# A fused macaron layer: the first unit's exponentials of its first 512 queries beside the last of its own maxima, and the opening's pieces in another order

## The chip, the cores and the metric

The kernel runs on one core of one Trainium2 chip. The metric is the device time of one execution in microseconds; before the change the median of four runs is 1354.56 us.

## The reference

Input x has 8 batches of 1024 rows of 256 values. The layer is feed-forward (a mixture of 8 experts with a capacity), attention, feed-forward, each on the normalized x and added to it:

```python
x = x + 0.5 * ffn(layernorm(x), gate_w, w1, b1, w2, b2)
x = x + attn(layernorm(x), Wq, bq, Wkv, bkv, Wo, bo)
x = x + 0.5 * ffn(layernorm(x), gate_w, w1, b1, w2, b2)

# attn: 16 heads of 16
q = x @ Wq.T + bq
k, v = split(x @ Wkv.T + bkv, 2)
dots = einsum('bhid,bhjd->bhij', q * scale, k)
dots = where(causal, MASK_VAL, dots)
out = einsum('bhij,bhjd->bhid', softmax(dots), v)
return out @ Wo.T + bo

# ffn: top 2 of 8 experts; an expert that more rows ask for than its capacity
# gives none of them anything
counts = bincount(a_e, length=E)
keep = counts <= cap
contrib = y[a_e, p] * (a_w * keep[a_e])[:, None]
```

An expert with more rows than its capacity adds nothing. The kernel counts the rows of each expert on the chip and runs a feed-forward layer only if some expert of it is kept; in the profiled execution none is, and the time is that of the attention and of the counting.

## The kernel before

**Units.** The attention works in 32 units, one for each batch `b` and group `g` of four heads: unit u = 4b + g. A unit needs the transposed queries and keys of its heads, `qT` and `kT` (128 x 1024, each head on a block of 32 partitions, 16 of them used and one more in each block holding a row of its own). There are four of each, taken in turn.

**Three kinds of work in a unit.** `m_steps(u)` gives 24 steps on the maxima: in each, for two heads (h = 0, 1), TensorE multiplies 128 queries by up to 512 keys into a score buffer `sm`, and VectorE reduces it along the row, straight with the causal mask (a custom instruction that writes `top`) or first to a partial maximum `first` where a row of blocks is wider than 512. Steps 0 to 7 are queries 0 to 511 (blocks 3, 2, 1, 0, two steps each, 512 to 128 keys wide), steps 8 to 15 the first 512 keys of queries 512 to 1023, steps 16 to 23 their remaining keys (512 to 128 wide). `settle(u, hf)` turns the maxima of one half of the queries on VectorE (`turned`), writes them to DRAM (`top_d`) and, three steps later, reads them back as one row in each block of `qT`; both are DMAs of SP, and the second waits for the first. With that row in `qT`, and -1 in the matching row of `kT` (a fill from `row16`), the products that `e_steps(u)` makes come out with the maximum taken away. `e_steps(u)` gives 24 steps also: for half 0 of the queries key blocks 0 to 3 (two steps each, 512 to 128 queries wide), for half 1 key blocks 0 to 7. In a step, for two heads, TensorE makes the products `sc`, ScalarE the exponentials into `pT`, GpSimd masks the diagonal block; two and three steps later TensorE multiplies `pT` by the values `vaug` into `pav`.

**The loop.** `for u in range(-1, NU)`: in unit u the scores of unit u lie beside the maxima of unit u + 1, a step of each at a time, so that the four row groups of TensorE hold two score and two maxima products. Stage u = -1 has only the maxima of unit 0 and takes two of their steps at a time; the last unit has only scores. All score buffers, `sm` and `sc`, come from six PSUM buffers in turn.

**Pieces.** `Beside` holds generators of further work. At every step the loop calls `beside.step(kinds)`: first whatever is due by its count of steps, then the second half of an open piece (`REST`), then the first work that asks for one of the kinds, in the order given (`QK` for projections, `PIECE` for the rest). `project(u)` makes the queries and keys of unit u: two halves of 512 rows, each two pieces of matmuls (`pq`), a copy on ScalarE (`packed`) and eight DMAs of 32 KB on SP (for unit 0 four of the eight are issued by ScalarE). `values_of(b, ...)` makes the values: two pieces of matmuls (`pv`) and two copies for each of eight blocks of 128 rows. `weights` (the generator `turning`) turns the weights: the first two parts before the loop, the gate and the value weights as first pieces, the rest in unit 0. `prepare` loads the next batch's x and takes its row statistics on VectorE.

**The opening** (lines 1142 to 1189): the loads of x in two halves of four blocks, statistics of both halves, then for each half the four normalized blocks `xn` (VectorE), two groups of four transposes (`turned`, `pta`, copied by ScalarE to `xnT`), and `project(0)` of that half. The `kT` fills of `kTs[:2]` stand before all this on ScalarE, those of `kTs[2:]` after it. Then

```python
opening = beside.add(chain(some(turning, 2), project(1), values_of(0, 0, 0, HT)))
```

and the other four blocks of values come in unit 0, ahead of all other pieces. In stage -1 there are two calls of `beside.step` after each pair of maxima steps, in unit 0 one call per step, with `(PIECE, QK)`.

**Order.** PE, VectorE, ScalarE and GpSimd compute in the order of the program (class `InOrder` ties each instruction to the one before). DMA issues are not tied: each issuing queue runs in one fixed order, which the framework chose when it built the program; in the trace the loads of the next two batches stand on SP at 9.01 us, far ahead of their place in the code. `bank` is a pair of PSUM buffers shared by `pta`, `pq`, `pv`, `pav` and the turned weights.

Of the kernel before, what the change touches and what calls it, by code (L numbers as in the profile page):

```python
# [13 lines left out]
ALU = mybir.AluOpType  # L14
# [4 lines left out]
P = 128  # L19
# [30 lines left out]
PIECE, QK, REST = "piece", "qk", "rest"  # L50


class Beside:
# [26 lines left out]
    def step(self, kinds=(), rest=True):  # L80
        self.now += 1
        self.due()
        if self.open is not None:
            if rest:
                self.advance(self.open)
            return
        for kind in kinds:
            for work in self.works:
                if work[1] == kind:
                    self.advance(work)  # L90
                    return
# [12 lines left out]
def macaron_kernel(  # L104
# [17 lines left out]
    B, S, D = x.shape  # L122
# [3 lines left out]
    TB = S // P  # L126
    DC = D // P
    NH = 16
    HD = D // NH
# [6 lines left out]
    QSCALE = HD ** -0.5  # L136
# [44 lines left out]
    row16 = const.tile([P, 1], F32, name="row16")  # L181
# [142 lines left out]
    def ln_rstd(mv, what, std=None):  # L324
        n = mv.shape[1]
        ve = norm.tile([P, TB], F32, tag="ve", name=f"ve_{what}")
        gpsimd.tensor_scalar(ve[:, :n], mv[:, :, 1], EPS, None, ALU.add)
        rstd = norm.tile([P, TB], F32, tag="rstd", name=f"rstd_{what}")
        gpsimd.tensor_tensor(rstd[:, :n], ve[:, :n], half[:, :n], ALU.pow)
        if std is not None:  # L330
            gpsimd.tensor_tensor(std, ve[:, :n], rstd[:, :n], ALU.mult)
        return rstd
# [351 lines left out]
    def attention(run_no, src, dst, gate0, logits, tally):  # L684
# [3 lines left out]
        with stack:  # L688
# [51 lines left out]
                yield 2  # L740


            def turned(b, jj, xns):
                pt = bank(f"pta{b}_{jj}")
                for i, xn in enumerate(xns):
                    for c in range(DC):
                        o = (c * 2 + i) * P
                        transpose(pt[:, o : o + P], xn[:, c * P : (c + 1) * P])
                scalar.copy(
                    xnTs[b][:, :, 2 * jj * P : (2 * jj + 2) * P], pt.rearrange("p (c w) -> p c w", c=DC)  # L750
                )

# [376 lines left out]
            def drain(steps):  # L1129
                for _ in steps:  # L1130
                    pass

            def some(steps, n):
                for _ in range(n):
                    ask = next(steps, None)
                    if ask is None:
                        return
                    yield ask
# [14 lines left out]
            qTs = [fixed.tile([P, S], F32, name=f"qT{run_no}_{k}") for k in range(4)]  # L1153
            kTs = [fixed.tile([P, S], F32, name=f"kT{run_no}_{k}") for k in range(4)]
            vaugs = [fixed.tile([P, TB, NH * VW + 32 - VW], F32, name=f"vaug{run_no}_{k}") for k in range(2)]
            gpsimd.memset(qTs[0], 0.0)
            for kT in kTs[:2]:
                scalar.copy(kT, row16.to_broadcast([P, S]))
            turning = weights(ap, bank, matmul, transpose) if gate0 is not None else iter(())
            next(turning, None)  # L1160
            next(turning, None)
# [1 line left out]
            stds[0] = norm.tile([P, TB], F32, tag="std", name="std0")  # L1163
            xnTs[0] = ap.tile([P, DC, S], F32, tag="xnT", name="xnT0", bufs=1)
            rstds = []
            for j0 in (0, HT):
                for j in range(j0, j0 + HT):
                    ln_stats(xb, j, st, mv)
                part = slice(j0, j0 + HT)
                rstds.append(ln_rstd(mv[:, part, :], f"a0_{j0}", stds[0][:, part]))  # L1170
            if gate0 is not None:
                gpsimd.tensor_scalar(bkqT[64:], bkqT[64:], QSCALE, None, ALU.mult)
            for qT in qTs[1:]:
                gpsimd.memset(qT, 0.0)
            for vaug in vaugs:
                gpsimd.memset(vaug[:, :, : NH * VW].rearrange("p t (h r) -> p t h r", r=VW)[:, :, :, HD:], 1.0)
                gpsimd.memset(vaug[:, :, NH * VW :], 1.0)
            for hf in range(2):
                xns = []
                for j in range(HT):  # L1180
                    xn = norm.tile([P, D], F32, tag="xn", name=f"xn_a0_{hf}_{j}", bufs=8)
                    ln_apply(xn, xb, hf * HT + j, mv, rstds[hf][:, j : j + 1])
                    xns.append(xn)
                for jj in range(2):
                    turned(0, 2 * hf + jj, xns[2 * jj : 2 * jj + 2])
                drain(project(0, (hf * 512,)))
            for kT in kTs[2:]:
                scalar.copy(kT, row16.to_broadcast([P, S]))
            beside = Beside()
            opening = beside.add(chain(some(turning, 2), project(1), values_of(0, 0, 0, HT)))  # L1190
            owed, adds, light, last, ons = deque(), deque(), deque(), [], {}
            STEPS = 24

# [1 line left out]
            for u in range(-1, NU):  # L1195
                b, g = divmod(u, NG)
                if u == 0:
                    beside.finish(opening)
                    preparing = beside.add(prepare(1, 2, 2))
                    opening = beside.add(values_of(0, 0, HT, TB), first=True)  # L1200
                    projecting = beside.add(project(2))
                    beside.add(chain((PIECE,), turning, residual(0)))
                if u >= 0 and g == 2 and b + 1 < B:
# [12 lines left out]
                if u > 0 and g == 0:  # L1216
                    beside.finish(valuing)
                ms = list(m_steps(u + 1)) if u + 1 < NU else [None] * STEPS
                es = list(e_steps(u)) if u >= 0 else []
                for k in range(0, STEPS, 2) if u < 0 else ():  # L1220

                    for h in range(2):
                        ms[k](h)
                        ms[k + 1](h)
                    if k == 8:
                        beside.add(settle(0, 0), first=True)
                    for _ in range(2):
                        beside.step((QK, PIECE))
                for k in range(0, STEPS, 2) if u == NU - 1 else ():

                    then = es[k + 1][1]
# [17 lines left out]
                    for kinds in ((PIECE,), ()):  # L1249
                        if light:  # L1250
                            light.popleft()()
                        beside.step(kinds)
                for k in range(STEPS) if 0 <= u < NU - 1 else ():


                    scores, then = es[k]
                    for h in range(2):
                        scores(h)
                        if ms[k] is not None:
                            ms[k](h)  # L1260
                    now = u * STEPS + k
                    if then is not None:
                        owed.append((now + 2, then, 0))
                        owed.append((now + 3, then, 1))
                    while owed and owed[0][0] <= now:
                        _, then, part = owed.popleft()
                        then(part)


                    if adds and 8 <= k <= 16:  # L1270
                        add_row()
                    if light and 8 <= k < 16 and g in (1, 2):
                        light.popleft()()
                    if u == NU - 2 and k in (0, 3):
                        beside.add(leave_first(b, k // 3))
                    if u == NU - 2 and k == 9:
                        dividing = beside.add(divided(b, 0, 8, 12, ons[0][:, 1], (2, 3, 3, 3)))
                    if g == 3 and k == 9:

                        beside.add(leave(b, 0))  # L1280
                    if g == 3 and k == 8:
                        beside.add(gate_first(b))
                    if g == 0 and b and k == 2:
                        beside.add(leave(b - 1, 1))
                    if g == 0 and b and k == 9:
                        beside.add(residual(b))
                    if g == 2 and b and k == 9:
                        beside.add(regate(b - 1, 0, TB))
                    if g == 1 and k == 7 and b + 1 < B:

                        beside.finish(preparing)
                        entering = beside.add(enter(b + 1), first=True)
                    if u == 0 and k == 15:
                        beside.finish(opening)
                    if k == 9 and ms[k] is not None:
                        beside.add(settle(u + 1, 0), first=True)
                    if k == 0:
                        settling = beside.add(settle(u, 1), first=True)
                    if k == 6:
                        beside.finish(settling)  # L1300
                    if u == 0:
                        beside.step((PIECE, QK))
                    elif g != 1 and u < NU - 2 and k not in (0, 8):

                        beside.step((PIECE,) if k in (2, 10, 13, 17) else (), k not in (14, 18))
                    elif k in (0, 8):
                        beside.step((QK, PIECE))
                    else:
                        beside.step((PIECE,) if k in long_steps or beside.pending() > 1 else ())
# [75 lines left out]
```

## Time and profile before

| | |
|---|---|
| median of 4 runs | 1354.56 us (1354.2 to 1356.48) |
| profiled execution | 1352.08 us, span 1350.20 us |
| mean granted TensorE clock | 0.989 |
| PE, matmul | 1315.1 us busy, 97% |
| DVE | 1015.4 us, 75% |
| ACT | 807.6 us, 60% |
| POOL | 440.1 us, 33% |
| first `sm` matmul (stage -1) | 24.58 us |
| first `sc` matmul (unit 0) | 52.35 us |
| first `sc` matmul of unit 0's step 8 | 68.22 us |
| first `sc` matmul of unit 1 | 99.01 us |

Times are microseconds from the start of the span. PE is TensorE's matmuls, PEld its weight loads, DVE VectorE, ACT ScalarE, POOL GpSimd, SPq the DMA issues of SyncE. Matmuls are pipelined and their ends are modelled: a matmul that waits in the queue can read as busy. A line of a timeline gives start, duration, engine, line, operation, output and inputs by name, count, and in brackets how long the engine was idle before it and what ended that. L37 is the line of the helper that records nearly every instruction, so groups are told apart by tile names.

### The profile page before, as it was taken

What the parts mean: (1) busy time and instruction counts of PE and PEld (TensorE: products, weight loads), DVE (VectorE), ACT (ScalarE), POOL (GpSimd) and SP (SyncE); (2) the same over time, 40 slices, a digit from 0 to 9 for tenths busy, and PEclk for the clock granted to TensorE, in tenths of its full rate; (3) what the DMA queues carried; (4) which work ended last, traced back from release to release, by engine and by line L of the source; (5) the groups of instructions that cost most, each with busy time, mean ns of one, the idle gap of its engine ahead of it and who ended that gap; (6) DMA issues with size and microseconds to landing.
All of it is one profiled execution on the core that took longest, in us unless ns stands there. A gap on an engine that the chain in (4) does not pass through costs nothing.

```text
span 1350.2 us, 51515 instructions
## 1 busy us (share of the span) xinstructions
PE 1315.1 (97%) x20664; PEld 437.0 (32%) x20664; DVE 1015.4 (75%) x3297; ACT 807.6 (60%) x1910; POOL 440.1 (33%) x776
## 2 busy tenths in 40 slices
PE   5999999999999999999999999999999999999994
PEld 2333333333333333333333333333333333333331
DVE  4876677778777788877778777777787777877865
ACT  3256666566666666666666666656666666666562
POOL 3034113442146221452125521354214622143321
PEclk9899999999999999999999999999999999999997
DMA  5011112212111121222122221211221111122201
GB/s 146 18 27 43 43 37 61 60 43 74 55 54 61 53 61 50 61 59 58 52 59 62 58 75 37 62 58 50 66 60 54 57 52 32 48 60 59 63 24 34
DMA packets 67024, 73.73 MB, mean 55 GB/s; under 512 B 24688, under 2 KB 42232, under 8 KB 66776
## 3 DMA queue, kind: packets, MB, share of 16 engines
q1 hardware_dynamic: 65432, 69.56, 17.8%
q8 instruction: 165, 2.70, 0.9%
q10 hardware_dynamic: 1344, 0.79, 0.2%
q14 instruction: 83, 0.68, 0.2%
HBM read 26.87 MB, written 26.20 MB: 39 GB/s over the span
## 4 chain that ended last, share of the span: by engine, by line
PE 95%; DVE 2%; issue 1%; ACT 1%; POOL 0%; DMA 0%; ACTq 0%; DVEq 0%; POOLq 0%
PE sc L37 42%; PE pav L37 24%; PE pq L37 9%; PE sm L37 8%; PE pv L37 5%; PE px L37 4%; PE pta L37 1%; DVE first L37 1%; ACT kT L37 0%; PE px_last L37 0%; DVE st_g L37 0%; ACTq L845 0%; DVE cand_g L37 0%; DVE xa L37 0%; DMA sums<-att_d 0%
## 5 line engine op out<-in xcount | busy, mean ns | idle before, releaser
L37 ACT ACTIVATE pT<-sc 128x512 f32<-128x512 f32 (+3 forms) x1536 | 669.2, 489 | 472.4 <-PE sm L37 356.2
L37 PE MATMUL sm<-kT,qT 32*64 32x512 f32 (+3 forms) x6144 | 731.4, 508 | 0.1
L37 PE MATMUL sc<-qT,kT 32*64 32x512 f32 (+3 forms) x6144 | 693.6, 507 | 0.0
L37 POOL TENSOR_SCALAR_AFFINE_SELECT pT<-pT 128x256 f32<-128x256 f32 x512 | 207.6, 407 | 786.5 <-ACT pT L37 778.9
L37 PE MATMUL pav<-pT,vaug 128*32 128x160 f32 (+4 forms) x5120 | 382.0, 370 | 2.8 <-POOL pT L37 2.0
L37 DVE TENSOR_REDUCE first<-sm 128x1 f32<-128x512 f32 x512 | 328.1, 684 | 75.1 <-PE sm L37 68.9
L37 DVE CUSTOM_DVE_ANT_0 sm<-sm,causal 128x256 f32<-128x256 f32 (+3 forms) x512 | 242.5, 516 | 131.2 <-PE sm L37 122.5
L37 DVE CUSTOM_DVE_ANT_0 sm<-sm,causal,first 128x256 f32<-128x256 f32 (+3 forms) x512 | 261.9, 557 | 84.6 <-PE sm L37 72.5
L37 PEld LDWEIGHTS sc<-qT,kT 32*64 32x64 f32 x6144 | 183.1, 130 | 368.9 <-ACT pT L37 303.7
L37 PEld LDWEIGHTS pav<-pT,vaug 128*32 128x32 f32 x5120 | 102.3, 108 | 362.2 <-issue 268.9
L37 PEld LDWEIGHTS sm<-kT,qT 32*64 32x64 f32 x6144 | 205.6, 130 | 17.7 <-DVE first L37 6.2
L37 DVE DVE_READ_ACCUMULATOR2_ANT top<- 128x1 f32 x1024 | 145.7, 142 | 0.0
L37 PE MATMUL pq<-xnT,wkqT 128*32 128x512 f32 x1024 | 137.2, 612 | 4.7 <-ACT xnT L37 3.2
L37 PE MATMUL pv<-wvT,xnT 128*32 128x264 f32 x1024 | 81.1, 392 | 0.0
L37 PE MATMUL px<-woT,on 128*32 128x264 f32 x960 | 76.2, 389 | 0.2 <-DVE xa L37 0.2
L37 POOL TENSOR_SCALAR xn_a<-xa,mv_a,rstd_a 128x256 f32<-128x256 f32 x56 | 67.8, 1221 | 0.0
L37 POOL TENSOR_TENSOR xa<-row,xa 128x264 f32<-128x264 f32 x56 | 41.8, 746 | 50.1 <-ACT row L37 50.1
L37 ACT ACTIVATE packed<-pq,bkqT 128x512 f32<-128x512 f32 x64 | 45.4, 709 | 11.1 <-PE pq L37 11.1
L37 POOL TENSOR_TENSOR xa<-xa,bo_all 128x528 f32<-128x528 f32 x32 | 41.4, 1313 | 14.5 <-issue 13.9
L37 PEld LDWEIGHTS pq<-xnT,wkqT 128*32 128x32 f32 x1024 | 25.9, 110 | 58.5 <-issue 52.4
L37 POOL TENSOR_TENSOR on<-on,inv 128x512 f32<-128x512 f32 (+1 forms) x32 | 40.3, 1280 | 10.7 <-DMA inv<-inv_d 10.7
L37 PEld LDWEIGHTS pv<-wvT,xnT 128*32 128x32 f32 x1024 | 29.8, 110 | 28.5 <-ACT att L37 14.1
(124 smaller groups left out, 454.5 us busy)
## 6 DMA issues: line engine op xcount, KB each, us to landing
att_d<-att SPq DMA_DIRECT2D x62, 256.0 KB
qT<-packed SPq DMA_DIRECT2D x256, 32.0 KB
out_dram<-xa SPq DMA_DIRECT2D x16, 512.0 KB
kT<-packed SPq DMA_DIRECT2D x248, 32.0 KB
on<-att_d SPq DMA_DIRECT2D x30, 256.0 KB
inv<-inv_d SPq DMA_DIRECT2D x30, 256.0 KB
xa<-in_L_attn_x_dram SPq DMA_DIRECT2D x7, 1024.0 KB
xa<-in_L_attn_x_dram SPq DMA_DIRECT2D x2, 512.0 KB
```

Of the source, the lines that this page charges most:

```text
L37: i = call(*args, **kwargs)
```

## The change

Unit 0's first eight score steps (queries 0 to 511) move from unit 0 into stage -1, beside steps 14 to 21 of unit 0's maxima; steps 0 to 13 and 22, 23 stay in pairs. In unit 0 the first eight steps then have only unit 1's maxima, in four pairs; steps 8 to 23 are as before. `settle(0, 0)` is asked for after step 7, `settle(0, 1)` after step 1 of unit 0 (step 0 before). Stage -1 calls `beside.step` 24 times as before, but asks for no piece in steps 14 to 19. In the opening chain the first values come before `project(1)`, the other four blocks of values may begin in stage -1, and unit 0's first eight steps ask for `(QK, PIECE)` instead of `(PIECE, QK)`.

In the opening the first half's blocks are normalized after six blocks' statistics, not eight; all `xn` are made before the transposes; the last two turned copies go to VectorE; the fills of `kTs[:2]` come after the first two turned copies and those of `kTs[2:]` at step 7 of stage -1; all four `qT` fills come first on GpSimd.

```diff
@@ -740,13 +740,13 @@
                 yield 2
 
 
-            def turned(b, jj, xns):
+            def turned(b, jj, xns, copy=scalar.copy):
                 pt = bank(f"pta{b}_{jj}")
                 for i, xn in enumerate(xns):
                     for c in range(DC):
                         o = (c * 2 + i) * P
                         transpose(pt[:, o : o + P], xn[:, c * P : (c + 1) * P])
-                scalar.copy(
+                copy(
                     xnTs[b][:, :, 2 * jj * P : (2 * jj + 2) * P], pt.rearrange("p (c w) -> p c w", c=DC)
                 )
 
@@ -1153,9 +1153,8 @@
             qTs = [fixed.tile([P, S], F32, name=f"qT{run_no}_{k}") for k in range(4)]
             kTs = [fixed.tile([P, S], F32, name=f"kT{run_no}_{k}") for k in range(4)]
             vaugs = [fixed.tile([P, TB, NH * VW + 32 - VW], F32, name=f"vaug{run_no}_{k}") for k in range(2)]
-            gpsimd.memset(qTs[0], 0.0)
-            for kT in kTs[:2]:
-                scalar.copy(kT, row16.to_broadcast([P, S]))
+            for qT in qTs:
+                gpsimd.memset(qT, 0.0)
             turning = weights(ap, bank, matmul, transpose) if gate0 is not None else iter(())
             next(turning, None)
             next(turning, None)
@@ -1163,31 +1162,48 @@
             stds[0] = norm.tile([P, TB], F32, tag="std", name="std0")
             xnTs[0] = ap.tile([P, DC, S], F32, tag="xnT", name="xnT0", bufs=1)
             rstds = []
-            for j0 in (0, HT):
-                for j in range(j0, j0 + HT):
+
+            def stats(j0, j1):
+                for j in range(j0, j1):
                     ln_stats(xb, j, st, mv)
-                part = slice(j0, j0 + HT)
-                rstds.append(ln_rstd(mv[:, part, :], f"a0_{j0}", stds[0][:, part]))
-            if gate0 is not None:
-                gpsimd.tensor_scalar(bkqT[64:], bkqT[64:], QSCALE, None, ALU.mult)
-            for qT in qTs[1:]:
-                gpsimd.memset(qT, 0.0)
-            for vaug in vaugs:
-                gpsimd.memset(vaug[:, :, : NH * VW].rearrange("p t (h r) -> p t h r", r=VW)[:, :, :, HD:], 1.0)
-                gpsimd.memset(vaug[:, :, NH * VW :], 1.0)
-            for hf in range(2):
-                xns = []
+
+            def rstd_of(hf):
+                part = slice(hf * HT, hf * HT + HT)
+                rstds.append(ln_rstd(mv[:, part, :], f"a0_{hf}", stds[0][:, part]))
+
+            def normed(hf):
                 for j in range(HT):
                     xn = norm.tile([P, D], F32, tag="xn", name=f"xn_a0_{hf}_{j}", bufs=8)
                     ln_apply(xn, xb, hf * HT + j, mv, rstds[hf][:, j : j + 1])
                     xns.append(xn)
-                for jj in range(2):
-                    turned(0, 2 * hf + jj, xns[2 * jj : 2 * jj + 2])
-                drain(project(0, (hf * 512,)))
-            for kT in kTs[2:]:
+
+
+
+            xns = []
+            stats(0, HT)
+            rstd_of(0)
+            if gate0 is not None:
+                gpsimd.tensor_scalar(bkqT[64:], bkqT[64:], QSCALE, None, ALU.mult)
+            stats(HT, HT + 2)
+            normed(0)
+            stats(HT + 2, TB)
+            rstd_of(1)
+            normed(1)
+            for vaug in vaugs:
+                gpsimd.memset(vaug[:, :, : NH * VW].rearrange("p t (h r) -> p t h r", r=VW)[:, :, :, HD:], 1.0)
+                gpsimd.memset(vaug[:, :, NH * VW :], 1.0)
+            for jj in range(2):
+                turned(0, jj, xns[2 * jj : 2 * jj + 2])
+            for kT in kTs[:2]:
                 scalar.copy(kT, row16.to_broadcast([P, S]))
+            drain(project(0, (0,)))
+            for jj in range(2, TB // 2):
+                turned(0, jj, xns[2 * jj : 2 * jj + 2], vector.tensor_copy)
+            drain(project(0, (512,)))
             beside = Beside()
-            opening = beside.add(chain(some(turning, 2), project(1), values_of(0, 0, 0, HT)))
+            opening = beside.add(chain(some(turning, 2), values_of(0, 0, 0, HT), project(1)))
+            opened = beside.add(values_of(0, 0, HT, TB))
+            first_es = list(e_steps(0))
             owed, adds, light, last, ons = deque(), deque(), deque(), [], {}
             STEPS = 24
 
@@ -1197,7 +1213,6 @@
                 if u == 0:
                     beside.finish(opening)
                     preparing = beside.add(prepare(1, 2, 2))
-                    opening = beside.add(values_of(0, 0, HT, TB), first=True)
                     projecting = beside.add(project(2))
                     beside.add(chain((PIECE,), turning, residual(0)))
                 if u >= 0 and g == 2 and b + 1 < B:
@@ -1216,16 +1231,46 @@
                 if u > 0 and g == 0:
                     beside.finish(valuing)
                 ms = list(m_steps(u + 1)) if u + 1 < NU else [None] * STEPS
-                es = list(e_steps(u)) if u >= 0 else []
-                for k in range(0, STEPS, 2) if u < 0 else ():
-
+                es = first_es if u < 1 else list(e_steps(u))
+
+                def step(k, e):
+
+
+                    scores, then = es[e]
                     for h in range(2):
-                        ms[k](h)
-                        ms[k + 1](h)
-                    if k == 8:
+                        scores(h)
+                        if ms[k] is not None:
+                            ms[k](h)
+                    now = u * STEPS + k
+                    if then is not None:
+                        owed.append((now + 2, then, 0))
+                        owed.append((now + 3, then, 1))
+                    while owed and owed[0][0] <= now:
+                        _, then, part = owed.popleft()
+                        then(part)
+
+
+
+
+                for k in range(STEPS) if u < 0 else range(8) if u == 0 else ():
+                    if u < 0 and 14 <= k < 22:
+                        step(k, k - 14)
+                    elif k % 2 == 0:
+                        for h in range(2):
+                            ms[k](h)
+                            ms[k + 1](h)
+                    if u < 0 and k == 7:
                         beside.add(settle(0, 0), first=True)
-                    for _ in range(2):
-                        beside.step((QK, PIECE))
+                        for kT in kTs[2:]:
+                            scalar.copy(kT, row16.to_broadcast([P, S]))
+                    if u == 0 and k == 1:
+                        while owed:
+                            _, then, part = owed.popleft()
+                            then(part)
+                        settling = beside.add(settle(0, 1), first=True)
+                    if u == 0 and k == 7:
+                        beside.finish(settling)
+                    beside.step((QK, PIECE) if u == 0 or not 14 <= k < 20 else ())
                 for k in range(0, STEPS, 2) if u == NU - 1 else ():
 
                     then = es[k + 1][1]
@@ -1250,21 +1295,8 @@
                         if light:
                             light.popleft()()
                         beside.step(kinds)
-                for k in range(STEPS) if 0 <= u < NU - 1 else ():
-
-
-                    scores, then = es[k]
-                    for h in range(2):
-                        scores(h)
-                        if ms[k] is not None:
-                            ms[k](h)
-                    now = u * STEPS + k
-                    if then is not None:
-                        owed.append((now + 2, then, 0))
-                        owed.append((now + 3, then, 1))
-                    while owed and owed[0][0] <= now:
-                        _, then, part = owed.popleft()
-                        then(part)
+                for k in range(0 if u else 8, STEPS) if 0 <= u < NU - 1 else ():
+                    step(k, k)
 
 
                     if adds and 8 <= k <= 16:
@@ -1291,12 +1323,12 @@
                         beside.finish(preparing)
                         entering = beside.add(enter(b + 1), first=True)
                     if u == 0 and k == 15:
-                        beside.finish(opening)
+                        beside.finish(opened)
                     if k == 9 and ms[k] is not None:
                         beside.add(settle(u + 1, 0), first=True)
                     if k == 0:
                         settling = beside.add(settle(u, 1), first=True)
-                    if k == 6:
+                    if u and k == 6:
                         beside.finish(settling)
                     if u == 0:
                         beside.step((PIECE, QK))
```

## The prediction

> **What bounds the kernel now.** I read the page's chain of waits first, then windows over the first units, then the chain and the timeline of the first 100 us, then SP's queue.
>
> ```profile
> PE 95%; DVE 2%; issue 1%; ACT 1%; POOL 0%; DMA 0%; ACTq 0%; DVEq 0%; POOLq 0%
> ```
>
> PE ends nearly everything, so time that PE loses at the start is lost at the end; what the change can win lies before unit 1. The windows are stage u = -1 (24.60 to 52.35), unit 0's steps 0 to 7 (to 68.22), its steps 8 to 23 (to 99.00), and a piece for the clock. Columns: length, then PE, PEld, DVE, ACT, POOL busy, granted clock, DMA.
>
> ```profile
> 24.60:52.35 27.75, 26.22 (x299) 9.60 (x295) 23.53 (x72) 6.36 (x15) 0.00 (x0) 0.92 0.14 31
> 52.35:68.22 15.87, 15.87 (x236) 5.69 (x232) 10.95 (x49) 7.36 (x22) 3.27 (x9) 0.81 0.02 3
> 68.22:99.00 30.78, 30.78 (x434) 11.36 (x432) 22.14 (x62) 17.89 (x41) 10.85 (x17) 1.00 0.12 29
> 50.00:55.00 5.00, 5.00 (x42) 2.56 (x36) 3.98 (x22) 0.60 (x1) 0.00 (x0) 0.50 0.01 3
> ```
>
> PE reads as full in the first 99 us, but the timeline shows what that is worth: 80 matmuls spread over 10.34 us behind DVE, where 16 take 1.11 us elsewhere.
>
> ```profile
> 42.30 10.34 PE L37 MATMUL sm<-kT,qT 32*64 32x512 f32 x80
> 38.96 7.23 DVE L37 TENSOR_REDUCE first<-sm 128x1 f32<-128x512 f32 x12
> 20.67 0.58 ACT L37 COPY xnT<-pta 128x512 f32<-128x512 f32 x1 [2.13 <-DMA kT<-packed]
> 21.31 3.34 PE L37 MATMUL pq<-xnT,wkqT 128*32 128x512 f32 x16 [2.53 <-ACT xnT L37]
> ```
>
> So stage -1 is DVE's: ACT makes no exponential and PE waits for score buffers. Its second half (42.3 to 52.4) has no pieces left to fill PE, and the granted clock is at half until about 58.4 (0.50 in 50 to 55, 0.66 in 55 to 60). The last two lines are the opening's hole: the copy of turned rows stands behind ACT's four DMA issues, and the projection behind the copy.
>
> **The opening.** The first `xn` no longer waits for four row statistics but for two: 2 x 0.56 us sooner. ACT's two `kT` fills (1.99) go from in front of the weight copies to beside the projection, which covers them (3.64). So the first projection starts at some 12.45 (13.62 before) and ends at 16.1. POOL's three more memsets (3.07) come into its idle 3.4 us before `ve`; without that cover, their surplus would show. The last two turned copies go to DVE, idle there; I price them as ACT's 0.58. They end at about 18.2 instead of 21.25, and the second projection with them at 20.2 (1.92 at full clock) to 21.9 (3.6). The first half's DMAs are issued from 16.85, four on ACT (2.5), and land by some 21.3. So the maxima start at **21.6 (21.2 to 21.9)** instead of 24.58: 3.0 won.
>
> **Stage -1.** DVE's pitch per tile, from start to start in the timeline, is 0.65, 0.52, 0.38, 0.25 (512 to 128 wide), 0.60 (reduce), 0.67, 0.54, 0.40, 0.27 (with `first`): 4 x 1.80 + 16 x 0.60 + 4 x 1.88 + 0.2 = 24.5 us, as before. What is new is PE's work, by the chain (a 512-wide step is 0.57 + 0.39 there at 88, 0.47 + 0.31 with 384 beside 256 at 91, less below):
> - paired steps 0 to 13 and 22: 0.96, 0.80, 0.62, 0.45, 3 x 0.96, 0.45 = 6.2;
> - eight single steps with scores: 4 x 0.96, 2 x 0.80, 2 x 0.6 = 6.7;
> - their `pav` 0.41, 0.73, 0.46, 0.46, 0.57 = 2.6;
> - pieces: gate and weights 0.7, six `pv` x 0.95 = 5.7, four `pq` halves x 0.9 = 3.6.
>
> The sum is 25.5 at the chain's durations; at the timeline's busy durations (1.11, 0.90, 0.69, 0.47, `pv` 1.10, `pq` 1.92, `pav` 2.98) it is 28.8. I take the middle, 27.2. PE and DVE now bind together, so I add half of what the old stage lost beyond DVE's work (27.75 - 24.4 = 3.35): 28.9. The stage ends at 21.6 + 28.9 = **50.5** instead of 52.35, with eight more steps done. ACT's eight pairs of exponentials, 4 x (0.60 + 0.49 + 0.38 + 0.28) = 7.0, lie beside DVE's maxima, as do the two late `kT` fills (2.1). The first scores wait for `settle(0, 0)`: maxima ready about 30, DMA issues at 30 and 32, landed 34, wanted at some 36.5. PE's queue behind them (`sm`, `pq`) is not held.
>
> **Unit 0, steps 0 to 7** become four pairs of unit 1's maxima (2.8 to 3.2), four `pq` halves (3.6 to 3.8), two `pv` (1.9 to 2.2) and a `pav` (0.6): 8.9 to 9.8 on PE; DVE has 7.2 + 0.2 + three or four row statistics at 0.6, 9.2 to 9.8. I take 9.5: step 8 could start at **60.0** instead of 68.22.
>
> **The new wait.** Step 8 reads the second half of `qT`, whose row of maxima comes from `settle(0, 1)`. Before, settle followed step 0, project(2) came later, and 10 us lay between the row's DMA (58.31) and step 8. Now settle comes at step 1, project(2) at steps 0 to 3, and its 16 DMAs share SP. SP issues in order at 0.61 us each; the trace shows what that does:
>
> ```profile
> 115.19 0.56 SPq L889 DMA_DIRECT2D top_d<-turned  x1
> 115.85 0.42 SPq L961 DMA_DIRECT2D att_d<-att  x1
> 116.36 2.43 SPq L845 DMA_DIRECT2D kT<-packed  x4
> 118.83 2.48 SPq L845 DMA_DIRECT2D qT<-packed  x4
> 121.42 0.53 SPq L891 DMA_DIRECT2D qT<-top_d  x1
> ```
>
> Eight issues put the row's DMA 6.2 us behind `top_d`; alone it is 2.0 (43.10 to 45.16, 56.30 to 58.31). In the change the first `packed` is ready at 50.5 + 1.0 (pair) + 1.7 + 0.6 + 0.75 = 54.5, `top_d` at about the same time, `att_d` takes 0.4, eight issues end at 59.8, and the row lands 2.0 later (as `top_d` did): 61.8. **Step 8 waits 1.8 us.** Behind it on PE stand the scores, `sm` and pieces; DVE and ACT run dry. The ends: 0 if the row goes ahead of the eight (as at 103.68 in this trace, before the eight at 104.80); 6.8 if it goes behind all sixteen.
>
> The Trainium skill ("DMA: Bandwidth & Descriptors", "Issuing engines are not separate DMA queues") says that starting DMAs on several engines saves only the sequencer's issue time, usually small beside the transfer. By that rule the sixteen would hold nothing, and the time would be the 1342.8 of the rival below; the 6.2 us above speak against it here.
>
> **Unit 0, steps 8 to 23.** Before: 30.78, PE at full clock. Four `pq` halves have gone from here; steps with one took 2.52 and 2.36 in the chain, those without 1.67 to 1.77, so 0.75 to 1.04 each: 3.6 (3.0 to 4.2) less, 27.2. `turning`'s pieces stay.
>
> **Sum.** 61.8 + 27.2 = 89.0, against 99.00: **10.0 us**. From unit 1 on the work is the same. The profiled execution took 1352.08 (span 1350.20 plus 1.88 around it) and would become 1342.1; the median of the four runs, 1354.56, becomes **1344.6**. No change can be told apart within 0.2%, 2.7 us.
>
> **Rivals.**
> - *No wait at step 8* (the row before the eight, or transfers short): 60.0 + 27.2 = 87.2, 11.8 won, 1342.8. With every term at its low end and DVE binding (22.3 + 24.5 + 9.2 + 26.6 = 82.6) 16 us, 1338.2; for it speaks that the row's `top_d` is ready near the eight, against it that eight such issues did go first at 116.36.
> - *The row behind all sixteen*: it waits 5.0 more, and PE without work falls to half clock, 3.4 us of it (the window 20 to 25 has a mean of 0.66: 5 x 0.34 / 0.5) costing 1.7. Won 3.3 to 5.0, 1349.6 to 1351.3. The second eight are ready about 57.5, the row at 56.5: a near thing.
> - *Slower: settle(0, 0) behind project(1) on SP*, as the old queue had it (`top_d` at 43.10 although `turned` was ready at 39.04). Sixteen issues from 34.3 end at 44.1, the row is issued at 46.2 and lands at 48.2; the first scores want it at 36.5. PE stalls 11.9 us with the maxima queued behind it, and 1.7 go to the clock: 10.0 - 13.6 = 3.6 lost, 1358.2. It decides from a stall of 10 us, so only if nearly all sixteen go first. Against it: the row's DMA is ready at 32, `packed` at 34.3.
> - *The edits do nothing for the time*: if PE's stages were bounded by work alone. Then only the opening's 3.0 less the new wait of 1.8 would stay: 1353.4. Against it: 80 matmuls in 10.34 us.
>
> The Trainium skill ("TensorE: Matmul & The Clock Gate", "What's actually happening") puts the half clock after an idle window of about 3.4 us. Here the clock fell at about 48.1 (the window 45 to 50 has a mean of 0.81) while matmuls never paused that long, only thinned out to every 2.4 us per 16. By the rule the old stage would have lost nothing to it, and unit 0's first steps would win some 2 us less; the rows decide.
>
> **How the numbers follow.** Forecast (wait of some 2 us) 0.45; no wait 0.17; behind sixteen 0.24; slower by settle(0, 0) 0.08; next to nothing 0.06. Faster by over 0.2%: 0.45 + 0.17 + 0.19 (four fifths of the third) = 0.81. Within: 0.05 + 0.06 = 0.11. Slower: 0.08. The range goes from 1340.0, between the low ends, to 1352.5, past the third case; what is left out is the slower case and most of the last.
>
> **What would show it.** First `sm` matmul at 21 to 22; the turned copies on DVE; exponentials from about 37 to 48 in stage -1; granted clock at 1.0 from 45 to 60, where it was 0.50; unit 1's first `first` reduction near 63 instead of 69.41; the row's `qT` DMA behind eight others, PE waiting some 2 us for it; unit 1's first scores near 89. I am wrong if the single steps in stage -1 take over 2 us each, if SP's queue holds PE over 5 us, or if the win at 89 is gone later.

## The result, and the profile after

The changed kernel takes 1358.35 us (median of 49 runs) against 1354.89 (72 runs): slower, ratio 1.0019, 95% interval [1.0013, 1.0025]. The forecast was 1344.6 with a range of 1340.0 to 1352.5. Of the 49 runs 13 lie at 1351.4 to 1354.4 us with a mean granted clock of 0.987 to 0.989, and the other 36, with the profiled execution (1357.61 us, span 1355.8, clock 0.983) among their kind, at 1357.0 to 1360.4 with 0.982 to 0.986.

The page's chain of waits after has a member that it didn't have before, SP's issues, with a DMA behind it:

```profile
PE 94%; DVE 3%; SPq 1%; DMA 1%; issue 0%; ACT 0%; POOL 0%; ACTq 0%; DVEq 0%
```

The windows of the same stages: stage -1 from its first maxima on, unit 0's steps 0 to 7 with the wait for step 8, steps 8 to 23, and two pieces for the clock (columns as before: length, PE, PEld, DVE, ACT, POOL busy, clock, DMA).

```profile
20.36:51.54 31.18, 29.86 (x442) 11.23 (x441) 25.80 (x81) 13.07 (x33) 3.94 (x10) 1.00 0.14 30
51.54:69.99 18.45, 9.49 (x142) 3.23 (x141) 9.71 (x44) 3.87 (x10) 0.29 (x1) 0.86 0.19 46
69.99:103.70 33.71, 33.71 (x381) 13.53 (x381) 21.42 (x59) 15.29 (x35) 9.92 (x14) 0.77 0.01 2
65.00:70.00 5.00, 0.01 (x2) 0.04 (x2) 0.00 (x0) 0.00 (x0) 0.00 (x0) 0.50 0.19 41
75.00:80.00 5.00, 5.00 (x38) 3.34 (x46) 2.59 (x6) 1.66 (x6) 0.00 (x0) 0.50 0.03 5
```

Stage -1 is what the change promised: ACT works (13.07 against 6.36), the clock stays at 1.00, and eight score steps are done with it. The second line is the loss: 18.45 us long with 9.49 of PE. In the third the same steps 8 to 23 that took 30.78 with four projection halves in them take 33.71 without, at a mean clock of 0.77. SP's queue in the timeline shows the wait:

```profile
55.50 0.57 SPq L889 DMA_DIRECT2D top_d<-turned  x1
56.17 0.41 SPq L961 DMA_DIRECT2D att_d<-att  x1
56.67 3.58 SPq L845 DMA_DIRECT2D kT<-packed  x4
60.35 2.43 SPq L845 DMA_DIRECT2D qT<-packed  x4
62.88 2.43 SPq L845 DMA_DIRECT2D kT<-packed  x4
65.35 2.48 SPq L845 DMA_DIRECT2D qT<-packed  x4
67.93 0.53 SPq L891 DMA_DIRECT2D qT<-top_d  x1
```

The row of maxima is issued 12.4 us after `top_d`, behind all sixteen DMAs of project(2). PE waits for it (timeline, then the view of waits: us in total, times, longest):

```profile
69.99 1.12 PE L37 MATMUL sc<-qT,kT 32*64 32x512 f32 x2 [8.96 <-DMA qT<-top_d]
```

```profile
PE sc L37 <- DMA qT<-top_d: 9.0, 1, 9.0
```

The granted clock falls at 64.8 in that gap and is full again only at 85.3 (windows of 1 us have 0.90 in 64 to 65 and 0.86 in 85 to 86, those between 0.50): 20.5 us, of which 15.3 with PE at work. The opening came out better than forecast; its lines answer to the last two of the first timeline fence of the prediction:

```profile
17.16 1.29 DVE L37 COPY xnT<-pta 128x512 f32<-128x512 f32 x2 [1.82 <-PE pta L37]
18.50 1.92 PE L37 MATMUL pq<-xnT,wkqT 128*32 128x512 f32 x16 [0.89 <-DVE xnT L37]
20.36 2.06 PE L37 MATMUL sm<-kT,qT 32*64 32x512 f32 x16
```

Nearly all that differs lies before unit 1: from its first turned maxima to the end of the span it is 1248.8 us before (1350.2 - 101.38) and 1249.7 after (1355.8 - 106.13).

### The profile page after: what moved, and what is told of

The parts are those of the page before. It is cut to its first block, busy times and chain, and to the rows that moved or that the text cites. A ratio compares the mean times of both kernels' runs of the same rounds, so it can differ in the third digit from the quotient of the medians.

```text
span 1355.8 us, 51518 instructions
## 1 busy us (share of the span) xinstructions
PE 1315.6 (97%) x20664; PEld 439.2 (32%) x20664; DVE 1016.5 (75%) x3299; ACT 807.1 (60%) x1908; POOL 439.8 (32%) x776
## 4 chain that ended last, share of the span: by engine, by line
PE 94%; DVE 3%; SPq 1%; DMA 1%; issue 0%; ACT 0%; POOL 0%; ACTq 0%; DVEq 0%
PE sc L37 42%; PE pav L37 24%; PE pq L37 9%; PE sm L37 8%; PE pv L37 4%; PE px L37 4%; PE pta L37 1%; SPq L845 1%; DVE first L37 1%; DMA xa<-in_L_attn_x_dram 0%; ACTq L845 0%; PE px_last L37 0%; PE pg L37 0%; DVE st_g L37 0%; DVE xa L37 0%
```

## The experiments

**1. The row first.** Unit 0's steps 0 to 3 ask for values pieces first, so project(2) comes two pieces later and its DMAs behind the row. The work ahead of step 8 is the same.

```diff
-beside.step((QK, PIECE) if u == 0 or not 14 <= k < 20 else ())
+beside.step((PIECE, QK) if u == 0 and k < 4 else (QK, PIECE) if u == 0 or not 14 <= k < 20 else ())
```

> The changed kernel, but unit 0's steps 0 to 3 ask for values pieces before project(2), so that SP issues the row of maxima (qT<-top_d of settle(0, 1)) ahead of project(2)'s sixteen DMAs. The work before step 8 is the same. Theory A (the row behind sixteen issues, 67.93, lost all of the gain: a 9 us stall of PE and the half clock after it): the row is issued near 57.5, PE reaches step 8's scores near 61 without a wait, the granted clock stays at 1.0 from 45 to 100, unit 1's first scores come near 88 to 89 instead of 103.7, and the time is some 14 us under the changed kernel, 10 to 11 under the one before: about 1344. Theory B (what was won in stage -1 is given back later by work that PE has to do anyway): at most 3 us under the one before.

Measured: 1343.83 us against 1354.70, ratio 0.9927 [0.9912, 0.9943]. SP's queue and the windows of the same stages:

```profile
55.99 0.57 SPq L889 DMA_DIRECT2D top_d<-turned  x1
58.01 0.52 SPq L891 DMA_DIRECT2D qT<-top_d  x1
60.32 2.44 SPq L845 DMA_DIRECT2D kT<-packed  x4
```

```profile
20.73:51.96 31.23, 29.54 (x435) 11.01 (x431) 25.73 (x80) 13.08 (x33) 3.96 (x10) 1.00 0.14 29
51.96:62.31 10.35, 10.35 (x144) 3.62 (x140) 9.17 (x42) 2.95 (x9) 0.30 (x1) 1.00 0.11 35
62.31:89.80 27.49, 27.49 (x380) 10.23 (x379) 21.78 (x62) 15.82 (x37) 9.95 (x14) 1.00 0.09 20
```

Theory A holds, B falls (step 8 comes at 62.31 where 61 was expected, unit 1 at 89.80 where 88 to 89 was): with one order changed the change wins 10.9 us, and from 92.24 (first turned maxima of unit 1) to the end it is 1249.7 us again. The two kernels differ by 7.7 us at step 8 (69.99 against 62.31) and by 6.2 in steps 8 to 23 (33.71 against 27.49): 13.9, and 14.5 in the medians.

**2. The row on another queue.** Only the issuer of one DMA changes; SP's sixteen issues stay where they were.

```diff
-nc.sync.dma_start(
+(nc.gpsimd if (u, hf) == (0, 1) else nc.sync).dma_start(
     out=qTs[u % 4][HD::32, hf * 512 : hf * 512 + 512],
```

> The changed kernel, but the one DMA qT<-top_d of settle(0, 1) is issued by GpSimd instead of SyncE; the order of all other work is untouched. Theory A (the place in SP's queue is what holds step 8): the row is issued 2 us after top_d, near 57.5 to 58, lands by 60, and the time is as with the row first, 1344 to 1346. Rival (the row's transfer itself, or the sixteen transfers in flight beside it, is what is slow): the row lands some microseconds late although it is issued early, and 5 or more of the 9 us of waiting stay.

Measured: 1343.96 us, ratio 0.9924 [0.9909, 0.9940], the same as experiment 1. POOL's line of the timeline, and PE's first scores of step 8, which wait for nothing:

```profile
58.30 0.82 POOL L891 DMA_DIRECT2D qT<-top_d  x1 [7.69 <-PE sm L37]
61.35 0.64 PE L37 MATMUL sc<-qT,kT 32*64 32x512 f32 x2
```

The sixteen transfers run beside it and PE doesn't wait, though the profile's list of DMAs has 2.9 us from this issue to the landing, just before step 8 begins. It was the place in the issuing queue.

**3. The gap filled.** The stall stays, but PE runs 64 matmuls without a use in it.

```diff
+if u == 0 and k == 7:
+    for i in range(8):
+        matmul_cols(bank(f"filler{i}"), wkqT[:, i % 2, 0]..., xnTs[0][:, i % 2, :512])
```

> The changed kernel with the stall kept, but 64 matmuls without a use (128x512, some 7.5 us at full clock) put on PE after step 7, into the time in which it waits for the row. Theory A (the half clock after the stall costs a part of its own): step 8's scores still come at 70, but the clock stays at 1.0 afterwards, unit 1's first scores come near 97 instead of 103.7, and the time is 6 to 7 us under the changed kernel: 1351 to 1352. If the half clock had cost only the 1.7 us of the prediction: 1356 to 1357. If it costs nothing: 1358.

Measured: 1352.17 us (12 runs), ratio 0.9994 [0.9981, 1.0006]. In the profiled execution, windows and the first scores of step 8:

```profile
51.02:68.85 17.83, 16.61 (x208) 5.27 (x205) 9.78 (x44) 3.87 (x10) 0.30 (x1) 1.00 0.19 47
68.85:96.43 27.58, 27.58 (x379) 10.88 (x379) 21.29 (x59) 15.14 (x35) 9.94 (x14) 1.00 0.01 3
```

```profile
68.85 0.65 PE L37 MATMUL sc<-qT,kT 32*64 32x512 f32 x2 [1.22 <-DMA qT<-top_d]
```

Step 8 is nearly as late as in the changed kernel (68.85 against 69.99), but steps 8 to 23 take 27.58 us instead of 33.71: the half clock cost 6.1, not 1.7. Filling is no sure cure: 1.2 us of gap were left, and the twelve runs go from 1350.0 to 1358.1.

**4. The opening alone**, in the kernel before: the change's lines down to the second `drain`, then the late `kT` fills, the chain of pieces and the loop of before.

> The kernel before with the opening's edits alone (statistics of six blocks before the first normalization, turned copies of the second half on VectorE, fills moved); exponentials, pieces and settle stay as before. Theory A: first maxima near 20.4 instead of 24.58, and as stage -1 is bound by VectorE from there on, the whole shift stays: 3 to 4 us under the one before, 1351. Rival: the second half's DMAs and the weight copies on ScalarE hold the stage as late as before: within 1 us of the one before.

Measured: 1349.47 us (11 runs), ratio 0.9963 [0.9953, 0.9973]: 5.2 us by the medians. The first maxima (timeline):

```profile
20.11 2.19 PE L37 MATMUL sm<-kT,qT 32*64 32x512 f32 x16
```

4.5 us earlier than 24.58; step 8 comes at 64.20 instead of 68.22 and unit 1 at 94.92 instead of 98.94 (the timeline's time of its first `sc` matmul; the table above has 99.01), so 4.0 of the shift stay.

**5. Everything but the opening**: experiment 1 with the opening of the kernel before.

> The kernel with the row first, but with the opening of the kernel before: only the exponentials' move and the new order of pieces are left of the change. Theory A (the two gains add): first maxima near 24.6, everything after it 4 us later than in the kernel with the row first, time 1348 to 1349, 6 us under the one before. Rival (the moved exponentials have slack, so an earlier opening is hidden once they are moved): within 1.5 us of the kernel with the row first, 1344 to 1345.

Measured: 1350.16 us, ratio 0.9965 [0.9953, 0.9978]: over the 1348 to 1349 that theory A expected, but 5.8 under the runs of the kernel before that it was timed beside (1355.94), where 6 was expected. The two parts add: 5.2 for the opening (experiment 4) and 5.8 for the rest (this one, from 1355.94) are 11.0, and experiment 1 has both for 10.9. First maxima at 24.57, step 8 at 66.16 and unit 1 at 93.64, each 3.8 to 3.9 after experiment 1. The medians hold more than the traces place: the profiled execution of the kernel before (1352.08) lies 2.6 and 3.9 under the two medians of that kernel (1354.70 and 1355.94), and from trace to trace the opening wins 4.0 at unit 1's first scores and experiment 1 9.1 (98.94 against 89.80). Where the kernel before loses the rest in other executions, no trace shows.

**6. The row behind eight**: the order that the prediction took as the likeliest.

```diff
-beside.step((QK, PIECE) if u == 0 or not 14 <= k < 20 else ())
+beside.step((PIECE, QK) if u == 0 and 2 <= k < 6 else (QK, PIECE) if u == 0 or not 14 <= k < 20 else ())
```

> The changed kernel with project(2)'s second half asked for in steps 6 and 7 of unit 0 instead of 2 and 3 (values pieces in between), so that the row of maxima stands on SP behind eight of project(2)'s DMAs instead of sixteen: the order that the prediction took as the likeliest. Theory A (the wait is issue time): the row is issued near 62.8, lands 2 us later, PE reaches step 8 near 62 and waits 2 to 3 us, and with so short a gap the clock stays at 1.0: 2 to 3 us over the kernel with the row first, 1346 to 1347. Rival (any wait of PE here costs the clock as well): the granted clock falls to 0.5 for 10 us or more and the time is 1350 or more.

Measured: 1350.02 us (6 runs, 1345.5 to 1353.5), ratio 0.9959 [0.9943, 0.9974]. SP's line, step 8's scores, and two windows:

```profile
62.84 0.53 SPq L891 DMA_DIRECT2D qT<-top_d  x1
64.84 0.96 PE L37 MATMUL sc<-qT,kT 32*64 32x512 f32 x2 [2.76 <-DMA qT<-top_d]
```

```profile
65.00:70.00 5.00, 5.00 (x50) 2.69 (x47) 3.03 (x7) 2.23 (x5) 0.00 (x0) 0.66 0.21 46
70.00:75.00 5.00, 5.00 (x47) 2.44 (x38) 2.95 (x7) 2.37 (x6) 0.00 (x0) 0.69 0.04 8
```

The issue time was right to the tenth (62.84), the wait is 2.8 us, and theory A is wrong on the clock: it falls at 65.0, just after so short a gap, and again at 71.9, for two stretches of 3.4 us in the profiled execution (5 x 0.34 / 0.5 in the first window, 5 x 0.31 / 0.5 and a little after in the second). Steps 8 to 23 take 30.0 (64.84 to 94.83), 2.5 over experiment 1. How much of the 2.5 is the gap's is not shown: experiment 8 has such a stretch without a gap. The rival's 10 us are too many for this execution, but its time is what the median shows.

**7. The thin stretch of stage -1 filled**, in the kernel before, with eight matmuls without a use after each of the last six pairs of maxima.

```diff
+if k >= 12:
+    matmul_cols(bank(f"filler{k}"), wkqT[:, 0, 0]..., xnTs[0][:, 0, :512])
```

> The kernel before with eight 128x512 matmuls without a use (some 0.9 us) on PE after each of the last six pairs of maxima in stage -1, where PE waits for VectorE. Theory A (the half clock of 48.1 to 58.4 comes of thinned-out matmuls and costs unit 0's first steps): the clock stays at 1.0, stage -1 ends as before because VectorE sets it, steps 0 to 2 take some 1.8 us each instead of 3.2, and the time is 2 to 3 us under the one before: about 1352. Rival (the clock falls anyway, or those steps wait for something else): no gain, 1354 to 1356.

Measured: 1352.66 us, ratio 0.9981 [0.9972, 0.9991]. Windows of the stretch whose clock was 0.81 and 0.50, and of steps 0 to 7:

```profile
45.00:50.00 5.00, 5.00 (x52) 1.20 (x56) 5.00 (x11) 0.00 (x0) 0.00 (x0) 1.00 0.04 8
50.00:55.00 5.00, 5.00 (x64) 1.44 (x64) 5.00 (x26) 0.00 (x0) 0.00 (x0) 1.00 0.00 0
54.58:67.50 12.92, 12.92 (x236) 4.89 (x232) 9.88 (x43) 7.25 (x22) 3.27 (x9) 1.00 0.02 5
```

Adding useless work makes the old kernel faster, by 3.3 us in the medians (1355.94 before) and 2.6 by the ratio. The clock stays full, and the first three steps take 1.63, 1.95 and 1.42 us; but stage -1 ended 2.2 us later here (54.58), which was not expected. From trace to trace steps 0 to 7 win 3.0 us (12.92 against 15.87), 0.7 is left at unit 1's first scores (98.22 against 98.94) and 0.1 in the span (1350.1 against 1350.2); where the rest of the medians' gain lies is not shown. The move keeps the clock at 1.00 in this stretch too, so a part of what it wins is likely the clock that thin matmuls had cost; how much is not shown.

**8. The keys' second half on SP**: experiment 1, with project(0)'s second half issuing its key DMAs on SP, out of the way of the weight copies.

```diff
-(nc.scalar if u == 0 and k < 4 else nc.sync).dma_start(
+(nc.scalar if u == 0 and s0 == 0 and k < 4 else nc.sync).dma_start(
```

> The kernel with the row first, and project(0)'s second half issues its four key DMAs on SP instead of ScalarE, where they stand ahead of the copies of the gate and value weights that PE's first values piece waits for (1.2 us). Theory: weight copies end near 23.5 instead of 25.15, PE does not wait at 24 to 25, and as PE and VectorE bind together there, 0.5 to 1.2 us are won: 1342.6 to 1343.3. Rival: the later keys of the second half (all eight issues on SP, ending near 26) or VectorE take it back: no difference from the kernel with the row first.

Measured: 1342.88 us (4 runs) against 1355.94, ratio 0.9902 [0.9888, 0.9916]. The weight copy and the piece that waited for it (25.20 in the changed kernel):

```profile
22.98 0.58 ACT L37 COPY wvT<-pt_w 128x512 f32<-128x512 f32 x1 [0.41 <-PE pt_w L37]
23.71 1.10 PE L37 MATMUL pv<-wvT,xnT 128*32 128x264 f32 x16
```

Step 8 comes at 60.68, 1.6 us before experiment 1. In the profiled execution a stretch of half clock takes it back by unit 1 (89.70 against 89.80); the median is 0.95 under. The window of that stretch, and PE's timeline where the clock falls (at 66.7, by windows of 1 us):

```profile
65.00:70.00 5.00, 5.00 (x39) 2.45 (x38) 2.96 (x6) 2.41 (x6) 0.00 (x0) 0.67 0.25 53
```

```profile
65.34 0.61 PE L37 MATMUL pg<-gcT,bo_cols 128*128 128x8 f32 x4
65.80 1.04 PE L37 MATMUL pg<-gcT,wsb 128*128 128x8 f32 x8
66.77 1.12 PE L37 MATMUL sc<-qT,kT 32*64 32x512 f32 x2
```

No wait of PE stands before it, only twelve small matmuls of the gate (`pg`, 8 wide). Experiments 8 and 1 were timed beside different runs of the kernel before, so which is faster is not settled; both beat the two kernels of the case.

## Why the prediction was wrong, point by point

**The step that failed first: the wait for the row.** The prediction gave the row a wait of 1.8 us and the order behind sixteen a chance of 0.24, because it compared when things are ready on the chip: the row at 56.5, the second eight at 57.5. They were ready at 57.5 (55.50 + 2.0) and 58.1 (`packed` at 57.41 + 0.69), in the forecast order and about as near as forecast. But SP did not take what was ready: the row, ready at 57.5, was issued at 67.93, behind eight DMAs that were ready only at 58.1. The queue's order was fixed when the program was built, and there the row stood last; PE waited 9.0 us for it, and SP's queue holding PE over 5 us was the prediction's own sign of being wrong. The code has this order too: project(2)'s sixteen DMAs are made in steps 1 and 3 of unit 0, the row's in step 4, three steps after settle. The code is no sure guide (at 103.68 in the trace before, SP has the row ahead of eight that the code makes earlier), but the prediction did not count it, and 0.24 was too little for this case. What the builder reckoned with is not shown by any run.

**The term that was mis-sized: the clock.** For that rival the prediction added 1.7 us, one stretch of 3.4 us at half clock. Measured: 20.5 us at half clock, 6.1 us lost (experiment 3). For the wait it had 6.8 there; 9.0 was measured. With these two measured terms the prediction's own sum comes near the result: 11.8 won without a wait (its figure; experiment 1 won 10.9), less 9.0 of wait, less 6.1 for the clock, is 3.3 lost; the medians say 3.5. And the case held to be likeliest, built as experiment 6, came to a wait of 2.8 and 2.5 more in steps 8 to 23, not 1.8.

**The Trainium skill's rules, weighed in the prediction.** "DMA: Bandwidth & Descriptors" ("Issuing engines are not separate DMA queues") calls the sequencer's issue time usually small beside the transfer; here it decided the time: 12.4 us from `top_d` to the row on SP, 2.6 with the row on POOL (55.74 to 58.30). "TensorE: Matmul & The Clock Gate" ("What's actually happening") puts the half clock after an idle window of about 3.4 us and the full one after a busy one. Here it fell just after a gap of 2.8 us (experiment 6), in thin work without a gap of that length (at 48.1 in the kernel before, which experiment 7 took away) and with no wait of PE before it (experiment 8); and after the stall it took 15.3 us of work to come back. The measurements decide.

**What was right.** Stage -1 was VectorE's, and moving the exponentials there, with the new order of pieces and the row first, is worth 5.8 us (experiment 5). The opening was priced at 3.0 and gave 4.2 at the first maxima (20.36; all the turned copies and the projection at full clock came at the early end), 5.2 in the median. Stage -1 was priced at 28.9 and took 31.2: PE's busy time, 29.86, lay over the upper of its two sums, 28.8, and 1.2 us went to waiting for `wvT`. Steps 0 to 7 were priced at 9.5, which is what PE worked in the changed kernel before its wait (9.49), and took 10.35 in experiment 1; steps 8 to 23 were priced at 27.2 and took 27.5. Without the wait the prediction gave 1342.8, and that kernel ran at 1343.83. That the ends meet so closely is partly luck: the early opening and the long stage -1 offset each other, and at unit 1 the trace of experiment 1 is at 89.80, 2.6 after the 87.2 of the sum. Within 0.9 us nothing was given back after unit 1, and settle(0, 0), the slower rival, had no wait: its row was issued at 32.06, as forecast. Two of the prediction's figures do not follow from its own terms, without consequence: 48.2 - 36.5 is a stall of 11.7, not 11.9, and the steps that it names differ by 0.59 to 0.85 with a projection half, not by 0.75 to 1.04; experiment 1 gives 0.82 for each (30.78 - 27.49 over four).

## What to carry to other kernels

Before a wait is called short, look at what stands ahead of it in the issuing queue, in the order of the built program, and count issue times: a small transfer that the next stage needs must not stand behind a batch that nobody needs yet. Work for TensorE that is moved earlier is only won if the consumer's other inputs come earlier as well. And price a gap of TensorE with the clock that follows it, not with its length alone.

## What had not been expected of the hardware

After a gap of 9.0 us the granted clock stayed at half for 15.3 us in which PE reads as busy throughout. After one of 2.8 us it was at half for two separate stretches of 3.4 us, and the second may have nothing to do with the gap. It begins as the twelve `pg` matmuls end (70.45 to 71.95), as the stretch of experiment 8 does; in experiments 1, 2 and 3 the same matmuls (in experiment 1 at 66.96 to 68.47) pass at full clock. In the changed kernel they lie at 77.11 to 79.83, inside the half clock, and whether they prolong it is not shown. Why the clock comes back so late, and why one kernel's executions differ in it, stays open; no run here varied the moment at which the gap begins.
